# PSUM as one ring of eight places, and one VectorE maximum for two neighbouring places

## Chip, cores and metric

The kernel runs on one core of a Trainium2 chip. The metric is the device time of one execution in microseconds (us); lower is better. TensorE (PE) multiplies matrices and writes its results only to PSUM, an on-chip memory of eight banks, each of which holds one 128 x 512 fp32 tile. VectorE (DVE) and ScalarE (ACT) read PSUM and bring results to SBUF. GpSimd (POOL) works in SBUF.

## The reference

Two layers over x of shape (4, 512, 256), each with an attention over a context of the same shape and a feed-forward network behind it, both gated by tanh of a scalar and added to x. Cut to what matters here:

```
x = x + tanh(g_xattn[0]) * attention0(layernorm(x), ctx)   # 16 heads of 16, softmax with a bias of -0.1*|i-j|
x = x + tanh(g_ffn[0])   * ffn0(layernorm(x))              # ternary weights, relu, 256 -> 1024 -> 256
x = x + tanh(g_xattn[1]) * attention1(layernorm(x), ctx)   # 16 heads, relu on q, k and v
x = x + tanh(g_ffn[1])   * moe(layernorm(x))               # 4 experts, top 1, 256 -> 1024 -> 256, layer norm
# in each attention, for every batch b and head h:
scores  = q @ k.T / sqrt(16)                 # 512 x 512
weights = exp(scores - rowmax) / rowsum
out     = weights @ v
```

The row maximum of the scores is what the change is about: it must be known before the exponentials are taken.

## The kernel before

The attention of one layer and one batch is cut into four groups of four heads (`groups`, L396; 32 groups in all). Within a group, `NT` = 4 tiles of 128 rows make four units, so that the main loop (L1264) goes over 128 units and four before them.

For each unit two kinds of score products are made, each of a 32-row operand with a 512-column one into one whole PSUM bank:

- `maxima` (L505): q·k for one row tile and two heads (a pair). The tiles are named pm. VectorE takes the maximum along the 512 columns of each (L517, TENSOR_REDUCE, output m). A unit has two pairs, thus four tiles.
- `weights` (L521): k·q, with the maxima already subtracted from q, for one key tile and two heads. The tiles are named psc. ScalarE takes the exponential (L532, output p), and in the first layer GpSimd multiplies a block by the decay.

The maxima run six units (`LEAD`) ahead of the exponentials. `scores` (L540) puts one pair of each kind together into a quad. The four products of a quad use the four different 32-row groups of TensorE and so run at the same time; first all four are issued, then their readers ("drains"). A unit has two quads, that is, eight tiles.

After the two quads of a unit `slot(u)` (L1213) gives TensorE other work: the weighted sum of a finished group (`weighted`, L553, tile po), the transposed maxima (`shifted`, L568, pmT), the division by the row sums (`divided`, L614, pn), and steps of other chains (projections L456, feed-forward L640, routing L723, experts L1042), which have costs and due units written by hand. After the last unit (about 690 us on the trace) the experts' products (L1104, L1299) run to the end; there are no score pairs in that part.

The order on TensorE, VectorE, ScalarE and GpSimd is the order in which the program issues the instructions (`manual_schedule`, L55). Waits between engines are derived by the language from tiles and from the parts of them that are read and written. All PSUM tiles come from `bank_psum` (L64): a pool of eight buffers of one bank, and each call makes a new tile. Such a tile gives its bank back when its last reader is done; the next call takes the bank that has been free longest.

Of the kernel before, what the change touches and what calls it, by code (L numbers as in the profile page):

```python
# [11 lines left out]
F32 = mybir.dt.float32  # L12
U32 = mybir.dt.uint32
AF = mybir.ActivationFunctionType
ALU = mybir.AluOpType
AX = mybir.AxisListType
PSUM = bass.MemoryType.PSUM
ET = mybir.EngineType

P = 128  # L20
# [31 lines left out]
def flamingo_kernel(ctx: ExitStack, tc: tile.TileContext, t: dict, out: bass.AP):  # L52
    nc = tc.nc
# [5 lines left out]
    wts = ctx.enter_context(tc.tile_pool(name="wts", bufs=2))  # L59
    dram = ctx.enter_context(tc.tile_pool(name="dram", bufs=1, space=bass.MemoryType.DRAM))  # L60
    sml = ctx.enter_context(tc.tile_pool(name="sml", bufs=4))
    ps = ctx.enter_context(tc.tile_pool(name="ps", bufs=8, space=PSUM))

    def bank_psum(name):  # L64
        return ps.tile([P, 512], F32, tag="bank", name=name)


    x = [const.tile([P, NT, D], F32, tag=f"x{b}", name=f"x{b}") for b in range(B)]
# [190 lines left out]
    def output_bias():  # L259


        bvm = made["bvm"]
        pb = bank_psum("pbv")[:, 0:D]
        for c in range(NC):
            nc.tensor.matmul(
                pb, lhsT=bvm[:, c, :], rhs=wo0[:, c, :], start=(c == 0), stop=(c == NC - 1)
            )
        nc.vector.tensor_tensor(bo0, bo0, pb, ALU.add)
        nc.gpsimd.tensor_scalar(bo0, bo0, gx0, None, ALU.mult)


    def quantize(flat, name, by_two):
# [12 lines left out]
        def limits():  # L285
            tot = bank_psum(f"qtot_{name}")
            nc.tensor.matmul(tot[:, 0:1], lhsT=ones, rhs=part[:, 0:1], start=True, stop=True)

            mean = sml.tile([P, 1], F32, tag="qmean", name=f"qmean_{name}")
            nc.vector.tensor_scalar(mean, tot[:, 0:1], 1.0 / (D * FF), 1e-5, ALU.mult, ALU.add)  # L290
            nc.vector.tensor_scalar(thr[:, 0:1], mean, 0.5, None, ALU.mult)
            nc.vector.tensor_scalar(thr[:, 1:2], mean, -0.5, None, ALU.mult)
# [82 lines left out]
    def transposed(src, dst, name, alone=False):  # L375

        for c in range(NC):
            pt = bank_psum(f"pt_{name}{c}")
            for n in range(NT):
                nc.tensor.transpose(pt[:, ts(n, P)], src[:, n, ts(c, P)], ident)  # L380
            (nc.scalar.copy if alone or c == 0 else nc.vector.tensor_copy)(dst[:, c, :], pt)
# [119 lines left out]
    def score(out_, lhs, rhs, i, n):  # L501
        r = slice(i * HP, (i + 1) * HP)
        nc.tensor.matmul(out_, lhsT=lhs[r, ts(n, P)], rhs=rhs[r, :], start=True, stop=True)  # L503

    def maxima(v, pair):  # L505

        g = groups[v // NT]
        n = v % NT
        pm = [bank_psum(f"pm{v}{pair}{i}") for i in range(2)]
        for i in range(2):  # L510
            score(pm[i], qs[g], ks[g], 2 * pair + i, n)
        m = m_sb[g[0]][g[3]]
        r = SPARE[g[3]]

        def drain():
            for i in range(2):
                nc.vector.tensor_reduce(m[:, n, 2 * pair + i, r : r + 1], pm[i], AX.X, ALU.max)  # L517

        return drain

# [19 lines left out]
    def scores(u, vs):  # L540

        ms = [(maxima, v, pair) for v in vs for pair in range(2)]
        ws = [(weights, u, 1 - pair) for pair in range(2)] if 0 <= u < n_units else []
        while ms or ws:
            if ms and ws:
                quad = [ms.pop(0), ws.pop(0)]
            else:
                left = ms or ws
                quad = [left.pop(0), left.pop(0)]
            for drain in [f(w, pair) for f, w, pair in quad]:  # L550
                drain()
# [712 lines left out]
    for u in range(-NT, n_units):  # L1264
# [22 lines left out]
        if u in totals:  # L1287
            job, i = totals[u]
# [215 lines left out]
```

## Time and profile before

| | |
|---|---|
| three runs | 831.85, 833.33, 833.40 us; median 833.33 |
| the profiled execution | 831.85 us, its span from first to last instruction 830.1 us |
| mean granted TensorE clock | 0.994 |
| VectorE, maxima (L517) | 512 instructions, 683 ns each, 317.0 us busy |
| ScalarE, exponentials (L532) | 512 instructions, 601 ns each, 267.1 us busy |
| TensorE, scores (L503) | pm 263.1 us and psc 275.5 us busy |

How to read it: the profile lists each engine's busy time, and groups instructions by line, engine, operation and tile (output <- input). Records of one fp32 score product come in twos, so 512 products of pm show as 1024. "Idle before" is the time in which the engine stood before an instruction, with what ended it. PEld is the weight load that precedes a matmul. A matmul's record overlaps that of the one before it, since they are pipelined; so the start of the next one, and not the end of this one, shows the pace.

### The profile page before, as it was taken

The page shows a single profiled execution, that of the slowest core. Times are in us where ns is not written, and L with a number is a line of the kernel's source. Part 1 is how long each engine was busy: PE and PEld are TensorE (multiplying, and loading weights), DVE is VectorE, ACT ScalarE, POOL GpSimd, SP SyncE. Part 2 cuts the span into 40 slices and gives each one's busy share as a digit, 9 for nine tenths or more (in the row PEclk, how much of TensorE's full clock was granted, in tenths as well). Part 3 has the DMA queues.
Part 4 walks back from the last instruction along what each step waited for, and adds up shares of the span by engine and source line. Part 5 has one row for each costly group of instructions (what it writes and reads, how often), then busy time and mean ns, then how long its engine had stood idle before and what let it go on. Part 6 is the DMA issues. An engine that isn't in the chain of part 4 may idle for free. (4 is left out here: it accounts for less than half of the span.)

```text
span 830.1 us, 13595 instructions
## 1 busy us (share of the span) xinstructions
PE 805.9 (97%) x5220; PEld 450.6 (54%) x5220; DVE 565.7 (68%) x1258; ACT 430.2 (52%) x900; POOL 290.5 (35%) x453
## 2 busy tenths in 40 slices
PE   5999999999999999999999999999999999999995
PEld 3444444545454345644565444564444555899994
DVE  6768868765857686577854676557687764689443
ACT  2476655653546454455635566346756666533341
POOL 5548455624233253231011132002313431735722
PEclk9999999999999999999999999999999999999998
DMA  8200000000001000000000001000104222726820
GB/s 313 77 1 1 1 1 1 1 1 1 1 1 39 1 1 1 1 27 1 1 1 1 26 1 52 1 1 1 52 1 148 91 94 77 273 80 240 303 94 32
DMA packets 17712, 42.28 MB, mean 51 GB/s; under 512 B 2032, under 2 KB 12016, under 8 KB 15216
## 3 DMA queue, kind: packets, MB, share of 16 engines
q0 software_dynamic: 5104, 27.34, 9.4%
q1 hardware_dynamic: 12128, 13.54, 4.8%
q8 instruction: 41, 0.67, 0.3%
q10 hardware_dynamic: 416, 0.54, 0.2%
q14 instruction: 23, 0.19, 0.1%
HBM read 35.13 MB, written 6.29 MB: 50 GB/s over the span
## 5 line engine op out<-in xcount | busy, mean ns | idle before, releaser
L517 DVE TENSOR_REDUCE m<-pm 128x1 f32<-128x512 f32 x512 | 317.0, 683 | 109.1 <-PE psc L503 105.6
L532 ACT ACTIVATE p<-psc 128x512 f32<-128x512 f32 x512 | 267.1, 601 | 145.7 <-PE psc L503 143.5
L503 PE MATMUL psc<-q,k 32*128 32x512 f32 x1024 | 275.5, 624 | 0.0
L503 PE MATMUL pm<-k,q 32*128 32x512 f32 x1024 | 263.1, 617 | 1.5 <-ACT q L490 0.9
L535 POOL TENSOR_TENSOR p<-p,dec 128x256 f32<-128x256 f32 x128 | 94.9, 746 | 170.9 <-ACT p L532 170.9
L503 PEld LDWEIGHTS pm<-k,q 32*128 32x128 f32 x1024 | 92.8, 184 | 83.4 <-issue 48.1
L503 PEld LDWEIGHTS psc<-q,k 32*128 32x128 f32 x1024 | 105.7, 184 | 51.4 <-issue 27.7
L560 PE MATMUL po<-p,v 128*32 128x512 f32 x1024 | 116.5, 595 | 0.8 <-DVE m L517 0.8
L560 PEld LDWEIGHTS po<-p,v 128*32 128x32 f32 x1024 | 31.3, 109 | 80.9 <-issue 58.6
L1104 PE MATMUL pg<-xs,wg 128*128 128x128 f32 x608 | 71.6, 276 | 0.7 <-DVE m L517 0.7
L1104 PEld LDWEIGHTS pg<-xs,wg 128*128 128x128 f32 x608 | 69.8, 192 | 4.1 <-DVE m L517 1.7
L583 POOL TENSOR_TENSOR q<-q,mT 128x512 f32<-128x512 f32 x16 | 20.3, 1269 | 132.3 <-ACT mT L582 132.3
L1130 ACT ACTIVATE ha<-pg,wg 128x128 f32<-128x128 f32 x120 | 34.3, 368 | 52.5 <-PE pg L1104 52.5
L682 PE MATMUL ph<-xTf,w1q 128*128 128x512 f32 x128 | 60.0, 605 | 0.0
L566 ACT COPY oT<-po 128x512 f32<-128x512 f32 x32 | 18.7, 586 | 75.6 <-PE po L560 75.6
L1299 PE MATMUL pyf<-wo,ha 128*128 128x256 f32 x256 | 57.6, 379 | 0.0
L388 PE MATMUL py_f<-w2q,h 128*128 128x256 f32 x256 | 57.2, 381 | 0.0
L388 PEld LDWEIGHTS py_f<-w2q,h 128*128 128x128 f32 x256 | 48.0, 190 | 9.4 <-DVE m L517 3.0
L1299 PEld LDWEIGHTS pyf<-wo,ha 128*128 128x128 f32 x256 | 47.6, 190 | 5.9
L460 PE MATMUL pk<-cT,wk 128*128 128x512 f32 x68 | 35.3, 644 | 7.3 <-DMA cT<-in_ctxT_dram 7.3
L682 PEld LDWEIGHTS ph<-xTf,w1q 128*128 128x128 f32 x128 | 22.6, 189 | 30.3 <-issue 18.2
L393 DVE SCALAR_TENSOR_TENSOR x<-py_f,tg,x 128x512 f32<-128x512 f32 x8 | 6.0, 751 | 42.4 <-PE py_f L388 42.4
(259 smaller groups left out, 828.6 us busy)
## 6 DMA issues: line engine op xcount, KB each, us to landing
x<-in_x_dram SPq DMA_DIRECT2D x4, 512.0 KB, 8.5
rows_d<-xn_f SPq DMA_DIRECT2D x4, 512.0 KB, 3.0
rows_d<-x SPq DMA_DIRECT2D x4, 512.0 KB, 3.7
cT<-in_ctxT_dram SPq DMA_DIRECT2D x3, 512.0 KB, 9.6
w1q<-in_w_dram SPq DMA_DIRECT2D x1, 1024.0 KB, 8.8
w2q<-in_w_dram SPq DMA_DIRECT2D x1, 1024.0 KB, 11.2
wo<-in_wo_dram SPq DMA_DIRECT2D x2, 512.0 KB, 3.8
rows<-in_rows_dram SPq DMA_DIRECT2D x1, 640.0 KB, 9.2
```

The source lines that it names most:

```text
L388: nc.tensor.matmul(py[:, n, :], lhsT=operand(c, n0 + n), rhs=w[:, c, :], start=(c == 0), stop=(c == chunks - 1),)
L460: nc.tensor.matmul(pp, lhsT=attn_w[layer][w][:, c, ts(tt, P)], rhs=src[:, c, :], start=(c == 0), stop=(c == NC - 1),)
L503: nc.tensor.matmul(out_, lhsT=lhs[r, ts(n, P)], rhs=rhs[r, :], start=True, stop=True)
L517: nc.vector.tensor_reduce(m[:, n, 2 * pair + i, r : r + 1], pm[i], AX.X, ALU.max)
L532: nc.scalar.activation(p[:, i, :], psc[i], AF.Exp, scale=SCALE)
L535: nc.gpsimd.tensor_tensor(d, d, dec.unsqueeze(1).to_broadcast([P, 2, P]), ALU.mult)
L560: nc.tensor.matmul(po[i * HP : (i + 1) * HP, :], lhsT=v_sb[b % 2][0][:, kt, c0 : c0 + HP], rhs=ps_exp[NT * s + kt, i // 2][:, i % 2, :], s ...
L583: nc.gpsimd.tensor_tensor(q2s[g], qs[g], turned, ALU.subtract)
L682: nc.tensor.matmul(ph, lhsT=w1q[:, c, ts(f, P)], rhs=st["xT"][:, c, :], start=(c == 0), stop=(c == NC - 1),)
L1104: nc.tensor.matmul(ph[:, f, :], lhsT=w[:, c, ts(f2 * NF // 2 + f, P)], rhs=xs[j][:, c, :], start=(c == 0), stop=(c == NC - 1),)
L1130: nc.scalar.activation(ha[:, f, :], (ha if src is None else src)[:, f, :], AF.Gelu, bias=biases[j][:, fa : fa + 1],)
L1299: nc.tensor.matmul(py, lhsT=hs[j, f // 4][:, f % 4, :], rhs=wo1[f // 4][:, f % 4, :], start=(f == 0), stop=(f == NF - 1),)
```

## The change

All PSUM now belongs to one tile `ring` of 128 x 8 x 512. `bank_psum` hands out its eight places in turn, and `two_banks` hands out two in succession for a pair of maxima, with a view over both. VectorE reads that view with one instruction that writes two columns of m. If the turn falls on place 7, the pair has places 7 and 0; the view is then the ring with a step of seven, and the two products are swapped, so that each head's maximum lands in its column. All other users of PSUM keep their code and get a slice of the ring in place of a tile of their own.

```diff
-    ps = ctx.enter_context(tc.tile_pool(name="ps", bufs=8, space=PSUM))
+    ps = ctx.enter_context(tc.tile_pool(name="ps", bufs=1, space=PSUM))
+
+
+    ring = ps.tile([P, 8, 512], F32, name="ring")
+    turn_of = [0]
 
     def bank_psum(name):
-        return ps.tile([P, 512], F32, tag="bank", name=name)
+        i = turn_of[0]
+        turn_of[0] = (i + 1) % 8
+        return ring[:, i, :]
+
+    def two_banks(name):
+
+        i = turn_of[0]
+        both = [bank_psum(name) for _ in range(2)]
+        if i == 7:
+            return both[::-1], ring[:, 0:8:7, :]
+        return both, ring[:, i : i + 2, :]
...
-        pm = [bank_psum(f"pm{v}{pair}{i}") for i in range(2)]
+        pm, both = two_banks(f"pm{v}{pair}")
         for i in range(2):
             score(pm[i], qs[g], ks[g], 2 * pair + i, n)
         m = m_sb[g[0]][g[3]]
         r = SPARE[g[3]]
 
         def drain():
-            for i in range(2):
-                nc.vector.tensor_reduce(m[:, n, 2 * pair + i, r : r + 1], pm[i], AX.X, ALU.max)
+            nc.vector.tensor_reduce(m[:, n, 2 * pair : 2 * pair + 2, r], both, AX.X, ALU.max)
```

## The prediction

> **What bounds the kernel now.** I read the page's first part, then a table by stretches of the span, then TensorE's own waits, and last the timeline of single units, on TensorE and on VectorE.
>
> ```profile
> span 830.1 us, 13595 instructions
> PE 805.9 (97%) x5220; PEld 450.6 (54%) x5220; DVE 565.7 (68%) x1258; ACT 430.2 (52%) x900; POOL 290.5 (35%) x453
> ...
> 45.00:680.00 635.00, 631.82 (x4012) 312.36 (x4005) 441.73 (x843) 350.17 (x670) 202.97 (x291) 1.00 0.05 18
> ```
>
> In the attention stretch (45 to 680 us; columns: length, then busy time of PE, PEld, DVE, ACT, POOL, then the granted clock) TensorE is idle for 3.2 of 635 us, at full clock, while VectorE is idle for 193 us. Time taken from VectorE is therefore worth little by itself; time in which TensorE has to wait is added to the end. TensorE's waits say the same:
>
> ```profile
> PE pk L460 <- DMA cT<-in_ctxT_dram: 7.3, 1, 7.3
> PE pmT L574 <- DVE m L517: 1.9, 1, 1.9
> PE pm L503 <- ACT q L490: 0.9, 1, 0.9
> PE po L560 <- DVE m L517: 0.8, 2, 0.5
> PE pg L1104 <- DVE m L517: 0.7, 2, 0.4
> PE pn L620 <- DVE m L517: 0.6, 1, 0.6
> ```
>
> With one more row of 0.5 (pm on m), all that TensorE waits for the maxima is 4.5 us. But how near these waits are to biting is seen in one unit (PE, then DVE, then PEld rows):
>
> ```profile
> 477.10 0.70 PE L503 MATMUL pm<-k,q 32*128 32x512 f32 x2
> 477.11 0.70 PE L503 MATMUL psc<-q,k 32*128 32x512 f32 x2
> ...
> 478.07 0.59 PE L503 MATMUL pm<-k,q 32*128 32x512 f32 x2
> ...
> 479.02 1.13 PE L682 MATMUL ph<-xTf,w1q 128*128 128x512 f32 x2
> ...
> 478.25 1.89 DVE L517 TENSOR_REDUCE m<-pm 128x1 f32<-128x512 f32 x3 [0.35 <-PE psc L503]
> ...
> 479.02 0.30 PEld L682 LDWEIGHTS ph<-xTf,w1q 128*128 128x128 f32 x2 [0.76 <-DVE m L517]
> ```
>
> A unit's scores take two quads of four products (two pm, two psc) and so all eight places. The quad at 477.10 is full at 478.23; VectorE begins its maxima at 478.25. The next job (ph) needs a ninth place, the first pm's. That reduction ends at about 478.93, and ph starts at 479.02, released by it. There is no slack left: the first place comes back just in time because it is reduced alone.
>
> **The change, part by part.**
>
> *VectorE's work.* 512 reductions of 512 elements become 256 of 1024. No row has 1024. The rows of the same operation by shape give the slope:
>
> ```profile
> L517 DVE TENSOR_REDUCE m<-pm 128x1 f32<-128x512 f32 x512 | 317.0, 683 | 109.1 <-PE psc L503 105.6 <-PE pm L503 3.2
> L904 DVE TENSOR_REDUCE edge_d<-key_d 128x1 f32<-128x4 f32 x6 | 0.8, 156 | 0.0
> ```
>
> (683 - 156) / 508 = 1.037 ns an element, so 1024 elements take 156 + 1020 x 1.037 = 1.214 us. Two single ones take 1.28 us from first start to last end (they overlap by 0.08). So a pair ends 0.07 us sooner, and 256 x 0.07 = 18 us leaves VectorE's row. The Trainium skill (VectorE: DVE Perf Modes, "Rules for kernel authors") says to minimise the count of VectorE instructions, because each pays its own drain. By that rule and the row, each instruction saved is worth the fixed 0.15 us, 38 us in all; by the overlap seen in the trace it is 18 us of an engine with 193 us to spare. On the path it can buy no more than TensorE's 4.5 us of waits. I take 1 us.
>
> *The first place of a pair comes back later.* The merged reduction gives both places back together, 1.214 us after its start, where the first came back after 0.68. In the unit above: 478.25 + 1.21 + 0.06 (release to restart: the trace shows 0.04 for a matmul, 0.14 where weights are loaded first) = 479.53 against 479.02, so TensorE stands 0.51 us. I did this for every TensorE instruction of the changed kernel as it is built: which reduction it waits for, when that would end on the trace of before, and when the instruction started there. Apart from the wrapped pairs below, 77 places are late by 0.18 to 0.53 us, with a sum near 35 us (some 50 of them at 0.47 to 0.53, the bare length of the second half); another 23 are late by 0.07 to 0.11 (2 us), which an earlier stall in the same unit mostly absorbs; two at 613.6 and 625.4, where VectorE is behind with the router's small steps, are late by 2.5 and 1.8, and I count half. Together 38 us. Nothing lies beside it: every later matmul is queued behind the waiting one.
>
> *The pair that wraps (places 7 and 0).* As built, 36 of the 256 pairs take places 7 and 0, and the view `ring[:, 0:8:7, :]` is treated as if it covered all eight places. The waits of the built program show it: such a reduction waits for the quad's last psc product and for ScalarE's last exponential, and the next TensorE instruction, whatever place it writes, waits for that reduction. ScalarE's exponentials of the same quad wait for it too. The other 220 pairs carry none of this.
>
> ```
> L530 TensorReduce m_146<-ring 128x2 [waits DVE_49,PE_49]
> L530 TensorReduce m_146<-ring 128x2 [waits DVE_49,PE_49,Activation_49]
> ```
>
> The price, from the unit at 399.44 us, one of the 36. Its quad's last product ends at 400.59; VectorE starts at 400.61, would end at 401.82, and TensorE goes on at 401.88. In the trace of before the next quad starts at 400.42 (matmuls overlap their predecessors' tails). Loss 1.46 us. The same reckoning at all 36:
> - 16 places at 1.46: 23.4 us;
> - 10 places where the pair is the unit's second, so that two reductions are still to be made, or VectorE is behind: 1.64 to 1.94, sum 17.5;
> - 10 places where TensorE's next instruction came later anyway: 0.85 to 1.42, sum 12.3.
>
> Sum 53 us. The waits on exponentials cost little of this: where ScalarE is last it is so by 0.4 us. The delayed exponentials (2 x 0.52 us) run while TensorE does its next quad, 0.97 us, and ScalarE is 52% busy; I cost them at nothing. If that cover failed, weighted sums (L560) would wait up to 1 us at some of the 32 groups.
>
> *Handing out places.* Before, a new tile takes the place released longest ago; now the one handed out longest ago. In the last 140 us, where there are no score pairs, only one instruction of the built order waits on something later than before (0.2 us). I count nothing.
>
> *The clock.* A standing TensorE can lose its clock. The trace has one case:
>
> ```profile
> 27.54 0.30 PE L574 MATMUL pmT<-ident,m 128*128 128x128 f32 x1 [1.94 <-DVE m L517]
> 25.26:28.67 3.41, 1.47 (x10) 1.16 (x8) 3.39 (x6) 0.00 (x0) 3.19 (x24) 1.00 0.03 7
> 28.67:32.08 3.41, 3.41 (x13) 1.61 (x15) 0.00 (x0) 0.59 (x1) 2.56 (x3) 0.50 0.03 7
> ```
>
> A 3.41 us stretch with TensorE busy for 1.47 us (43%) is followed by one at half clock. The skill (TensorE: Matmul & The Clock Gate, "Why this matters for your kernels") warns only of idle gaps over about 3 us; by it none of my stalls costs clock. By this row a gap of 1.94 us did. A stretch that was 78% busy (11.61 to 15.02 us, 2.65 us) kept the clock. A stall of 1.46 us inside one such stretch leaves it 57% busy, between the two. Bounds: none, or a half-clock stretch at about 20 of the 36 (the stall falls whole into one stretch in (3.41 - 1.46) / 3.41 = 57% of cases), each losing half of 3.41, 34 us. I take the low side, one or two cases, 2 us, since only the 1.9 us stalls come as low as the row that was punished; the high end stays in the range.
>
> *Sum.* 53 + 38 + 2 - 1 = 92, less 1 for startup, where TensorE waits at 27.5 us for VectorE anyway: 91 us. The profiled execution took 831.85 us (its span 830.1 and 1.7 around it); the median of the three runs is 833.33. So 922.9 for the profiled one, 924 for the median.
>
> **Rivals.**
> - *The clock falls at most wrapped pairs.* Against it: 57% is nearer the middle than the punished 43%. For it: no row between 43 and 78% shows a kept clock. 924 + 32 = 956 us.
> - *Only the wrapped pairs cost.* If TensorE's next job after the scores has enough of its own lead-in, or the merged reduction is shorter than the slope says, late first places vanish: 833 + 53 = 886 us. Against it: the PEld rows with 0.76 released by m, 28 of them at pmT alone.
> - *Only the late first places cost*, because the waits over all eight places are met when they are reached: 833 + 38 = 871 us. Against it: the waiting matmul directly follows the quad.
> - *Not slower.* VectorE is the hidden bound, and its 18 us shorten TensorE's waits for the maxima. Price: at most those 4.5 us, 829 us. It decides if TensorE, after a pair's scores, always has some 1.5 us of work into places that wait for nothing. The unit at 477 us shows 0.09 us of slack, and the wrap leaves no such place.
>
> **How the numbers follow.** Both kinds of stall as sized, 905 to 940: 0.58. Clock lost at many places, 940 to 975: 0.17. Wrapped pairs only, or first places half hidden, 875 to 905: 0.18. First places only, 855 to 875: 0.04. Not slower: 0.03. The range 890 to 957 holds about 0.8. Less than 0.2%, some 1.7 us, could not be told from no change; faster 0.02, the same 0.01, slower 0.97.
>
> **What would show it.** Right: the merged reduction at about 1.21 us, 256 of them; VectorE's busy sum near 548; TensorE's waits with new rows from the reduction, some 36 of 1.3 to 1.9 us and some 75 of about 0.5; TensorE busy still near 806 in a longer span. Wrong: granted clock below full through the attention stretch (then the clock rival); TensorE's waits on m only near 1.5 us long (the second); no wait on m over 1 us (the third). An error in the length of the merged reduction of 0.1 us moves the time by 11 us, since some 113 stalls contain it.

## The result, and the profile after

The changed kernel takes 930.75 us (median of four runs, 929.34 to 932.87) against 832.84 us before (four runs): a ratio of 1.118, 95% interval 1.116 to 1.119, or 98 us more. The prediction said 924 with a range of 890 to 957. Three later executions of 1141, 2005 and 2751 us, one of the kernel before and two of the last merged kernel, ran in a slow state and are left out of every figure.

The page of the changed kernel, first part, and the row of 45 to 680 us (columns as in the prediction):

```profile
span 928.1 us, 13394 instructions
PE 812.3 (88%) x5220; PEld 444.3 (48%) x5220; DVE 558.8 (60%) x1002; ACT 433.7 (47%) x900; POOL 289.8 (31%) x453
```

```profile
45.00:680.00 635.00, 559.76 (x3446) 267.22 (x3446) 378.65 (x501) 306.08 (x578) 179.24 (x262) 0.99 0.02 7
```

TensorE does the same 5220 matmuls. It was busy 805.9 of 830.1 us and is now busy 812.3 of 928.1: 91.6 us more idle time and 6.4 us more busy time, together the 98 us. In the stretch from 45 to 680 us it stands for 75 us where it stood for 3.2, and the attention now runs on to about 774 us. What it stands for is told by its own waits in the changed kernel (us in total, times, longest):

```profile
PE ring L517 <- DVE m L530: 40.1, 29, 2.1
PE ring L573 <- DVE m L530: 17.3, 19, 2.3
PE ring L587 <- DVE m L530: 13.9, 17, 1.8
PE ring L474 <- DMA cT<-in_ctxT_dram: 7.3, 1, 7.3
PE ring L474 <- DVE m L530: 6.3, 11, 1.6
PE ring L695 <- DVE m L530: 5.3, 12, 0.7
PE ring L443 <- DVE m L530: 3.2, 5, 1.4
PE ring L402 <- DVE m L530: 2.5, 6, 0.5
PE ring L394 <- DVE m L530: 2.3, 5, 0.6
PE ring L769 <- DVE m L530: 2.1, 2, 1.6
```

With four more rows of 0.5 us, TensorE waits 110 times for the maxima, 95.0 us against 4.5 before. The 90.5 us between them are nearly all of the new idle time. L517 is the line of the score products, L573 that of the weighted sums (L560 before), L587 that of the transposed maxima (L574).

One wrapped pair, in the timeline of the changed kernel (PE, DVE and ACT rows):

```profile
426.32 0.59 PE L517 MATMUL ring<-k,q 32*128 32x512 f32 x2
426.33 0.59 PE L517 MATMUL ring<-q,k 32*128 32x512 f32 x2
427.06 1.23 DVE L530 TENSOR_REDUCE m<-ring 128x2 f32<-128x1024 f32 x1 [0.42 <-PE ring L517]
...
428.35 0.70 PE L517 MATMUL ring<-k,q 32*128 32x512 f32 x2 [1.42 <-DVE m L530]
...
428.39 0.60 ACT L545 ACTIVATE p<-ring 128x512 f32<-128x512 f32 x1 [3.52 <-DVE m L530]
```

The quad ends at 426.92, the reduction runs from 427.06 to 428.29, and only then do TensorE and ScalarE go on, both released by it. In this trace 36 such waits last 1.39 to 2.14 us, 55.7 us in all. And one late first place, a little earlier in the same view:

```profile
420.88 2.36 DVE L530 TENSOR_REDUCE m<-ring 128x2 f32<-128x1024 f32 x2 [2.42 <-PE ring L517]
...
421.07 0.59 PE L517 MATMUL ring<-q,k 32*128 32x512 f32 x2
421.08 0.59 PE L517 MATMUL ring<-k,q 32*128 32x512 f32 x2
...
422.16 0.70 PE L695 MATMUL ring<-xTf,w1q 128*128 128x512 f32 x1 [0.48 <-DVE m L530]
```

The unit's two merged reductions start at 420.88. The first ends at 422.1 with both its places, and the next job, which needs the first of them, starts at 422.16 after 0.48 us of standing.

### The profile page after: what moved, and what is told of

Read it like the earlier page. It is cut to its first block, busy times and chain, and to the rows that moved or that the text cites. A ratio compares the mean times of both kernels' runs of the same rounds, so it can differ in the third digit from the quotient of the medians.

```text
span 928.1 us, 13394 instructions
## 1 busy us (share of the span) xinstructions
PE 812.3 (88%) x5220; PEld 444.3 (48%) x5220; DVE 558.8 (60%) x1002; ACT 433.7 (47%) x900; POOL 289.8 (31%) x453
## 5 line engine op out<-in xcount | busy, mean ns | idle before, releaser
L530 DVE TENSOR_REDUCE m<-ring 128x2 f32<-128x1024 f32 x256 | 304.6, 1222 | 180.9 <-PE ring L517 171.2
L545 ACT ACTIVATE p<-ring 128x512 f32<-128x512 f32 x512 | 270.0, 600 | 200.8 <-PE ring L517 136.2
L517 PE MATMUL ring<-k,q 32*128 32x512 f32 x1024 | 263.2, 625 | 40.2 <-DVE m L530 39.2
L517 PE MATMUL ring<-q,k 32*128 32x512 f32 x1024 | 276.4, 630 | 1.3 <-DVE m L530 1.0
L517 PEld LDWEIGHTS ring<-k,q 32*128 32x128 f32 x1024 | 86.0, 184 | 138.0 <-issue 68.8
L573 PE MATMUL ring<-p,v 128*32 128x512 f32 x1024 | 117.8, 600 | 18.1 <-DVE m L530 17.3
L517 PEld LDWEIGHTS ring<-q,k 32*128 32x128 f32 x1024 | 100.9, 184 | 43.4 <-issue 21.2
L573 PEld LDWEIGHTS ring<-p,v 128*32 128x32 f32 x1024 | 32.2, 110 | 100.0 <-issue 66.7
L1117 PE MATMUL ring<-xs,wg 128*128 128x128 f32 x608 | 72.1, 277 | 0.6 <-DVE m L530 0.5
L1117 PEld LDWEIGHTS ring<-xs,wg 128*128 128x128 f32 x608 | 70.5, 193 | 4.2 <-DVE m L530 1.3
L695 PE MATMUL ring<-xTf,w1q 128*128 128x512 f32 x128 | 61.6, 619 | 5.3 <-DVE m L530 5.3
L695 PEld LDWEIGHTS ring<-xTf,w1q 128*128 128x128 f32 x128 | 23.6, 198 | 36.9 <-issue 21.8
```

Of the source, the lines that this page charges most:

```text
L530: nc.vector.tensor_reduce(m[:, n, 2 * pair : 2 * pair + 2, r], both, AX.X, ALU.max)
L545: nc.scalar.activation(p[:, i, :], psc[i], AF.Exp, scale=SCALE)
L573: nc.tensor.matmul(po[i * HP : (i + 1) * HP, :], lhsT=v_sb[b % 2][0][:, kt, c0 : c0 + HP], rhs=ps_exp[NT * s + kt, i // 2][:, i % 2, :], s ...
L695: nc.tensor.matmul(ph, lhsT=w1q[:, c, ts(f, P)], rhs=st["xT"][:, c, :], start=(c == 0), stop=(c == NC - 1),)
L1117: nc.tensor.matmul(ph[:, f, :], lhsT=w[:, c, ts(f2 * NF // 2 + f, P)], rhs=xs[j][:, c, :], start=(c == 0), stop=(c == NC - 1),)
```

## The experiments

**Which part costs what?** My theory has two causes on two sets of places: the merged read gives its first place back late (every unit in which a job follows at once), and the wrapped view is guarded as if it covered all eight places. Its rivals: the ring as such costs, only one of the two counts, or the clock makes the difference. Four kernels take the parts singly. In all of them "two reads" is the loop of the kernel before, one reduction for each place. Each ratio is to runs of the kernel before in the same series: its median was 832.67 us beside the first three kernels and the one that hands out psc first, and 831.6 us beside the others.

*The ring alone.* The changed kernel with two reads for every pair:

```diff
-            nc.vector.tensor_reduce(m[:, n, 2 * pair : 2 * pair + 2, r], both, AX.X, ALU.max)
+            for i in range(2):
+                nc.vector.tensor_reduce(m[:, n, 2 * pair + i, r : r + 1], pm[i], AX.X, ALU.max)
```

> The ring is kept, and each pair's maxima are taken by two instructions again, so that no view covers two places. Theory (all the loss comes from the merged reads: places given back late, and the wrapped view that is treated as all eight places): 833 us, within 2 us of the kernel before, one half-clock stretch as there. Rival (handing out places in turn costs by itself, because a place can come up whose reader is late): some of the 98 us stays, 840 us or more, with TensorE waits that the kernel before does not have.

Measured: 841.7 us, ratio 1.0117 (1.0099 to 1.0135). That is a miss: 9 us where I expected none. TensorE's waits in it show the source, short waits of about 0.5 us that the kernel before did not have, and a few of over 1 us:

```profile
PE ring L588 <- DVE m L531: 5.4, 7, 1.9
PE ring L574 <- DVE m L531: 3.8, 5, 1.9
PE ring L402 <- DVE m L531: 1.0, 2, 0.5
PE ring L474 <- DVE m L531: 1.0, 2, 0.5
```

Thirteen waits of about 0.5 us, 6 us in all, are on place 7 of a wrapped pair. My edit left the pair swapped, so place 7, which the next job gets before place 0, was read second. That is a fault of this edit and not of the change, where a merged read returns both at once. Beside it two jobs wait 1.9 and 1.2 us (a weighted sum and a transposed maximum near 619 and 632 us). The kernel before does not wait there, so its pool had a free place to give; the strict turn gives one that VectorE has not yet read. A later kernel takes the swap out.

*Merged, but wrapped pairs read twice.*

```diff
+        wraps = turn_of[0] == 7
         pm, both = two_banks(f"pm{v}{pair}")
...
         def drain():
+            if not wraps:
+                nc.vector.tensor_reduce(m[:, n, 2 * pair : 2 * pair + 2, r], both, AX.X, ALU.max)
+                return
+            for i in range(2):
+                nc.vector.tensor_reduce(m[:, n, 2 * pair + i, r : r + 1], pm[i], AX.X, ALU.max)
```

> As changed, but the 36 wrapped pairs are read by two instructions; the other 220 stay merged. Theory: the stalls of about 1.5 us at the wrapped pairs fall to about nothing (such a pair gives its first place back early too), the 77 or so of 0.5 us stay: 867 to 876 us, and TensorE's waits on m near 40 us in all with none over 1 us except where VectorE is behind. Rival (the wrapped pairs are the whole loss, and the short stalls would be made up): 833 to 845 us. Rival (the clock is a large part): still over 885 us.

Measured: 874.6 us, ratio 1.0505 (1.0488 to 1.0523). The long waits on the wrapped pairs are gone and the short ones stay: 76 waits on a merged reduction of about 0.45 us each, 34.4 us in all. Five longer ones (7.4 us) have the two of the strict turn among them. Twelve waits of the swap (5.8 us) are in this kernel too.

*Only the wrapped pairs merged.* The same with `if wraps:` in place of `if not wraps:`.

> The other half: only the 36 wrapped pairs are merged, the other 220 are read by two instructions. Theory: 36 stalls of about 1.5 us and a few half-clock stretches: 885 to 895 us. Together with the run that leaves the wrapped pairs alone the losses should add up to the 98 us of the change within some 6 us. Rival (the strided view is merely read slowly): the wrapped reduction would have to be longer than 1.22 us; it was not in the changed kernel's trace. Rival (wrapped pairs cost only because VectorE is already late from the other merged ones): under 875 us.

Measured: 895.45 us, ratio 1.0773 (1.0738 to 1.0808), just above the 885 to 895 that I expected. The six rows of its waits on a merged reduction (L532) are these:

```profile
PE ring L517 <- DVE m L532: 37.6, 24, 2.5
PE ring L578 <- DVE m L532: 8.3, 5, 1.8
...
PE ring L592 <- DVE m L532: 5.8, 4, 1.7
...
PE ring L774 <- DVE m L532: 1.6, 1, 1.6
PE ring L474 <- DVE m L532: 1.6, 1, 1.6
PE ring L443 <- DVE m L532: 1.5, 1, 1.5
```

36 waits, 56.4 us: one for each wrapped pair. Only 36 of the 256 pairs are merged here, and they cost more than the other 220 did in the kernel above. The two losses, by the ratios 42 and 64 us, add up to 8 more than the 98, where I had allowed 6: what the ring costs by itself is in both, as the next kernel shows.

*The ring in order.* The first kernel once more, with the wrapped pair not swapped, so that place 7 is written and read first:

```diff
         if i == 7:
-            return both[::-1], ring[:, 0:8:7, :]
+            return both, None
```

> The ring with two reads a pair, and in a wrapped pair place 7 now holds the first product and is read first. The earlier run of the ring with two reads kept the swapped products, so that place 7, the next in turn, was read second: 13 of its TensorE waits, 6 us, are on place 7. Theory (those 6 us are the swap; the other 3 are the two jobs at 619 and 632 us for which the pool had picked a place freed earlier): 835 to 837 us. Rival (handing out in turn costs more at random places): still 840 or more.

Measured: 834.99 us, ratio 1.0043 (1.0028 to 1.0058), as expected. The strict turn itself costs some 3.6 us, most of it at the two places named above (1.9 and 1.2 us again). With the turn counted once and the swap's 6 us left out, the two losses above come to 97 us.

**The wrapped view, or the merged read at those places?** A wrapped pair differs from the others in its view, which is guarded as eight places, and in its place in the turn. This kernel is the ring in order, except that a pair whose turn falls on 7 leaves place 7 out and takes 0 and 1; only these 43 pairs are merged, over neighbouring places.

```diff
+        skips = turn_of[0] == 7
+        if skips:
+            turn_of[0] = 0
         pm, both = two_banks(f"pm{v}{pair}")
...
         def drain():
+            if skips:
+                nc.vector.tensor_reduce(m[:, n, 2 * pair : 2 * pair + 2, r], both, AX.X, ALU.max)
+                return
```

> Only the pairs whose turn falls on place 7 are merged, as in the run that merges the wrapped pairs alone (895 us), but place 7 is left out and they take places 0 and 1, so the view covers just the two (43 pairs here, since leaving places out shifts the turns). Theory (the wrapped pair's price is the wait over all eight places, not the merged read): at most 43 late first places of 0.5 us where the pair opens a unit, half of them: 836 + 11 to 22, with a little for turns with seven places: 845 to 860 us. Rival (a merged read costs 1.5 us at these pairs whatever its view): 890 us or more.

Measured: 856.56 us, ratio 1.03 (1.0283 to 1.0318), 21.6 us above the ring in order. The view over all eight is what costs 1.5 us a time: without it none of the 43 merged reads holds TensorE for more than 0.6 us but one (1.3 us, near the end). But only 17 of the 43 hold TensorE at all, for 8.4 us together; the other 13 of the 21.6 us are not among TensorE's waits. I laid the starts of each TensorE instruction in this trace beside those in the trace of the ring in order. Sixteen units, in which the next job waits for a merged read, take 8.6 us longer in all from their first score product to that job. The rest is the seven-place turn of this kernel: in fifteen units the unit's own last score product already needs the place of its first maximum, and these take 13.7 us longer. Together that is the 22.3 us between the two spans; what differs elsewhere cancels. The weight load of such a product:

```profile
226.28 0.29 PEld L517 LDWEIGHTS ring<-q,k 32*128 32x128 f32 x2 [0.70 <-DVE m L537]
```

VectorE's two single reductions of the same unit:

```profile
225.54 1.29 DVE L537 TENSOR_REDUCE m<-ring 128x1 f32<-128x512 f32 x2 [0.30 <-PE ring L517]
```

The first of them ends at about 226.23 and releases the load. On TensorE this delay does not show as idle time, because the other products of the quad are still running and the late one then runs on alone; it shows in the busy time, 820.6 us against 806.8 in the ring in order. So some 8 of the 21.6 us belong to merging and some 14 to this edit. The 845 to 860 us expected came true with other shares than expected: fewer late first places, and more of the seven-place turn than "a little".

**Can the late first place be hidden?** A unit's places are handed out maxima first. If the two psc products of a quad take the first places, the next job needs a place that ScalarE returns, and the maxima's places are wanted only two places later in the turn. On the kernel with two reads at the wrap:

```diff
-                quad = [ms.pop(0), ws.pop(0)]
+                quad = [ws.pop(0), ms.pop(0)]
```

> As the run with two reads at wrapped pairs, and the quad takes its two psc places before its two pm places, so that the ninth place after a unit's scores is one that ScalarE gives back after one exponential of 0.6 us. Theory (the short stall is the first pm place coming back late, and only because it is the next in turn): the stalls of 0.5 us vanish, 828 to 838 us. Rival (TensorE waits for the longer reduction wherever the pair stands, through the depth of eight places): 860 us or more.

Measured: 845.06 us, ratio 1.015 (1.0133 to 1.0167): better than 874.6 by 29.5 us, but not the 828 to 838 expected. The waits on m are nearly gone. In their place come thirteen waits on ScalarE's p, 14 us in all, ten of them of 1.2 us. One of them (ACT and PE rows):

```profile
212.84 0.58 ACT L584 COPY oT<-ring 128x512 f32<-128x512 f32 x1 [2.46 <-PE ring L578]
213.32 2.07 ACT L379 ACTIVATE xn_a<-x,off_a,rstd_a 128x256 f32<-128x256 f32 x4
215.30 1.54 ACT L550 ACTIVATE p<-ring 128x512 f32<-128x512 f32 x3
...
215.93 0.92 PE L402 MATMUL ring<-wo,o 128*128 128x256 f32 x3 [1.23 <-ACT p L550]
```

In each of the thirteen, ScalarE has just scaled the four row tiles of a layer norm (2.07 us), its exponentials come late, and now TensorE's next job needs their place. My expectation took ScalarE as free in every unit.

So the last two kernels hand out psc first, except in those units, where the maxima keep the first places and are read one by one; the wrapped pairs too are read one by one, in order. 201 pairs are merged and 110 reductions are single. The first added line stands in the layer norm, where the rows are scaled, and marks that ScalarE does it. The control is the kernel before, pool and two reads as they were, with the same order of the quad.

```diff
+            made["rows"] = eng is None
...
+        apart = turn_of[0] == 7 or made.get("late")
...
+        late = made["late"] = made.pop("rows", False)
...
-                quad = [ms.pop(0), ws.pop(0)]
+                quad = [ms.pop(0), ws.pop(0)] if late else [ws.pop(0), ms.pop(0)]
```

> Merged pairs, with two reads where the pair wraps; the quad takes psc places first, except in the unit after a layer norm whose four rows ScalarE scales (2.07 us, so that ScalarE comes late to its exponentials): there pm places come first and are read one by one. In the earlier run with psc first ten waits of 1.2 us were on ScalarE in just such units. Theory: these 12 us go, 831 to 835 us, no different from the kernel before by more than 0.3%, since TensorE has almost no waits left to give back. Rival (less VectorE work is worth something once nothing waits for it): under 830 us.

> The kernel before, one bank a tile and two reads a pair, with only the order in the quad changed as in the merged version: psc first except after a layer norm on ScalarE. Theory: 829 to 833 us; the difference to the merged version with the same order is what merging is worth when nothing waits for it, within 2 us of zero. Rival (merging is worth its 18 us of VectorE time in part): this one over 4 us slower than the merged version.

Measured: 832.6 us merged, ratio 1.0008 (0.9996 to 1.002), and 832.79 us for the control, ratio 1.0018 (1.0007 to 1.0029). In the merged one TensorE's waits for the maxima are down to a handful:

```profile
PE ring L594 <- DVE m L533: 1.8, 1, 1.8
...
PE ring L1033 <- DVE m L536: 0.3, 1, 0.3
...
PE ring L518 <- DVE m L533: 0.2, 1, 0.2
```

VectorE is busy for 559.5 us in it and for 571.6 in the control:

```profile
PE 807.0 (97%) x5220; PEld 451.5 (54%) x5220; DVE 559.5 (67%) x1057; ACT 428.1 (52%) x900; POOL 290.1 (35%) x453
```

```profile
PE 807.7 (97%) x5220; PEld 453.1 (55%) x5220; DVE 571.6 (69%) x1258; ACT 428.0 (52%) x900; POOL 290.3 (35%) x453
```

The 12 us that VectorE saves are worth nothing that can be measured: the intervals of the two ratios overlap, and TensorE is busy for 97% of both spans. A gain of some 2 us between them is not excluded. No version beats the kernel before (831.6 us beside these two).

## Why the prediction was right, point by point

The parts, in microseconds over the kernel before; the measured column is from the runs' ratios times 832.8:

| part | predicted | measured | from |
|---|---|---|---|
| wrapped pairs | 53 | 61, of which 56 are waits | only wrapped merged (1.0773) less ring in order (1.0043) |
| late first places (without the two at 613.6 and 625.4 us) | 36 | 32 | wrapped read twice (1.0505) less ring in order, less 6 of the swap |
| those two places; in the runs, the strict turn | 2 | 3.6 | ring in order (1.0043) |
| clock, in all | 2 | about 6, an estimate, within the rows above | busy time of PE, 812.3 - 805.9 |
| VectorE's gain | -1 | 0 | merged beside its control |
| startup | -1 | not seen by itself | |
| sum | 91 | 97 of the 98 | |

The sum is 7 us short of the 98. The wrapped pairs were put 8 us too low and the late first places 4 us too high; that these cancel in part is luck.

*What bounds the kernel.* Right: TensorE without slack, and VectorE's time worth little. The two last kernels show the second half of it by themselves.

*The merged reduction.* 1.214 us was worked out from the slope of two shapes; the changed kernel's row has 1.222. The wrapped view is read no slower than the others. Of all 256 the shortest, the median and the longest, in ns:

```profile
L530 DVE TENSOR_REDUCE m<-ring x256: 1192/1225/1228, 16.6 to 773.9; 128x2 f32<-128x1024 f32 x128
```

VectorE's reductions fell from 317.0 to 304.6 us:

```profile
L530 DVE TENSOR_REDUCE m<-ring 128x2 f32<-128x1024 f32 x256 | 304.6, 1222 | 180.9 <-PE ring L517 171.2
```

I had said 18 us less, and it was 12. I had reckoned every pair of single reductions as standing alone, 1.28 us, but pairs that follow each other overlap too: the row of before gives 317.0 / 256 = 1.238 for a pair, the row of after 304.6 / 256 = 1.190. Other work of VectorE takes 5 us more, so "VectorE's busy sum near 548" came out as 558.8. It did not matter. The Trainium skill's rule of fewer VectorE instructions (VectorE: DVE Perf Modes, "Rules for kernel authors") holds for the engine here, with 12 us, and not for the kernel, with none that could be measured.

*Late first places.* Right in mechanism and size. The changed trace has 74 waits on m besides the 36; they sum to 39.3 us, 4.5 of which were there before, and about 3 are the turn's. That leaves 32, as the difference of the runs does. One reading behind it was wrong, and harmless. "ph starts at 479.02, released by it" is not what the trace of before shows, and the weight loads with 0.76 before them are no waits. The same 0.76 stands before a load that nothing held, and the last record of the unit's score products starts 0.52 us before ph:

```profile
477.09 0.19 PEld L503 LDWEIGHTS pm<-k,q 32*128 32x128 f32 x2 [0.76 <-issue]
...
478.50 0.59 PE L503 MATMUL pm<-k,q 32*128 32x512 f32 x2
```

In that trace 110 jobs follow a unit's scores by these 0.52 us, so it is TensorE's own pace; the maximum had ended at 478.95, just before. The estimate stands because it was worked out from start times, which already held this pace.

*The two places at 613.6 and 625.4 us.* I took 2.5 and 1.8 us of lateness there, counted half (2 us), and put them down to the merged reads, with VectorE behind with the router's steps. That 3.6 us was measured in their place is luck. The ring with two reads shows that they are not the merged read's: 1.9 and 1.2 us of waiting appear with single reductions too. The step "I count nothing" for handing out places looked only at the last 140 us; in the attention stretch the turn does cost, which I had put at nothing, and its price stood in my sum under another name.

*Wrapped pairs.* Right in mechanism: 36 waits, and TensorE's next instruction whatever its place. Predicted 53 us; the trace has 55.7. I gave 0.85 to 1.94 us as the span of single costs; it is 1.39 to 2.14. The lower end was too low: it came from ten places, put at 12.3 us, where I took TensorE's next instruction to come later anyway. The exponentials' delay cost nothing, as said: ScalarE waits 54.8 us for m (its row follows), but no wait of TensorE for p is among the eighteen largest.

```profile
ACT p L545 <- DVE m L530: 54.8, 31, 4.0
```

*The clock.* This is the term that was mis-sized. I said one or two half-clock stretches. Beside one at the end of every span, the trace of before has one after its start-up, and the changed one has seven, each 3.4 us long. TensorE is busy for 21.8 us in these seven and for 3.4 in the one of before, so at half clock they can have cost at most 9 us more. The row of its busy time grew by 6.4, but that is no clean measure of the clock: in the kernel that leaves out place 7 busy time is 14 us above the ring in order, with one such stretch in each. I argued from the one row with 43% busy. Five stretches of the changed trace (columns as before); the first, second, fourth and fifth are followed by half clock, the third is not; the sixth row is what follows the first:

```profile
49.20:52.61 3.41, 1.27 (x12) 0.37 (x12) 1.23 (x1) 2.12 (x6) 1.26 (x1) 1.00 0.00 0
189.14:192.55 3.41, 1.54 (x12) 0.55 (x16) 1.94 (x2) 1.33 (x3) 0.00 (x0) 1.00 0.00 0
438.30:441.71 3.41, 1.71 (x20) 0.69 (x16) 2.67 (x3) 1.61 (x4) 0.83 (x5) 1.00 0.00 0
708.00:711.41 3.41, 1.96 (x12) 0.50 (x5) 3.31 (x7) 2.09 (x4) 0.00 (x0) 1.00 0.00 0
295.00:298.41 3.41, 2.14 (x12) 0.50 (x5) 3.11 (x3) 1.20 (x3) 0.72 (x1) 0.99 0.25 77
52.61:56.02 3.41, 3.08 (x16) 1.01 (x8) 1.37 (x2) 2.63 (x7) 1.51 (x3) 0.50 0.00 0
```

At 37%, 45%, 57% and 63% busy the clock fell, at 50% it held. The other three of the seven follow stretches of 45, 53 and 58%. If the whole trace is cut into such stretches, counted from the falls, twenty of 50 to 59%, the third row among them, kept full clock. And in the ring with two reads a stretch as busy as the 43% of before kept it too, as the row after it shows:

```profile
617.20:620.60 3.40, 1.46 (x17) 0.46 (x20) 3.21 (x11) 0.80 (x2) 0.00 (x0) 1.00 0.00 0
620.60:624.00 3.40, 3.40 (x36) 1.38 (x32) 1.20 (x7) 0.58 (x1) 0.00 (x0) 1.00 0.00 0
```

So the busy share of the stretch ahead does not decide by itself, and what else does stays open. The rival in which most wrapped pairs lose the clock is out: 7 stretches and not 20. The skill's rule (TensorE: Matmul & The Clock Gate, "Why this matters for your kernels"), with its gaps of over about 3 us, would have said none; the longest idle time of TensorE at these seven is 2.34 us.

*The rivals.* "Only wrapped pairs" (886) and "only late first places" (871) each got a kernel of their own, 895 and 875 (869 without the swap's 6 us): both parts are real, and each alone falls short of 931. "Not slower" fails by the same table.

*What stays open.* What decides whether the clock falls; and about 1 us between the sum of the parts and the whole, within what the intervals of the runs leave. How much of the measured 61 us of the wrapped pairs is clock is bounded only: the waits are 56.4, and TensorE's busy time is 810.2 us there against 806.8 in the ring in order.

## What to carry to other kernels

Before two reads of PSUM are joined into one, ask when the next writer needs the first of the two places: here that was at once for about a third of the pairs, and each of these cost TensorE up to the length of the second half, 0.5 us. A view with a step over a tile that is shared may be guarded as the whole tile, so look at what the built program's waits name, not at what the view reads. And an instruction saved on an engine with a third of its time idle bought nothing even when every new wait had been removed.

## What the hardware showed that I had not expected

A standing TensorE lost its clock although none of its waits on the maxima was over 2.34 us, after 3.41 us stretches of 37 to 63% busy; but most stretches of 50 to 59% kept it, and one of 43% was followed by half clock in one trace and by full clock in another. A reduction over two banks seven apart takes as long as over neighbours (at most 1.228 us, against a median of 1.225). And the order in which a quad's places are handed out is worth most of what merging the unwrapped pairs costs: the same merged kernel with psc first lost 29.5 us of its 42, because it is then ScalarE's place, and not VectorE's, that the next job needs.
